# Two fourth sums of a seven-product matrix scheme: from VectorE to accumulating transfers inside SBUF

## The chip, the cores and the metric

The kernel runs on one core of one Trainium2 chip. The core has TensorE (PE, matrix products into PSUM), VectorE (DVE, elementwise work), ScalarE (ACT, activations and copies), GpSimd (POOL, which here issues transfers that add to their target) and SyncE (SP, which issues the other transfers). Transfers from both queues run on the same 16 transfer engines. SBUF is the on-chip memory that all engines work in. The metric is the time on the device in microseconds (us), the median of several executions; lower is better.

## The reference

A two-layer graph attention network over 32 independent graphs of 512 nodes with 512 features, in float32:

```python
h = relu(layernorm(x))
mask = (adj > 0) | eye
# one layer: H heads of F features
xl   = (h @ W).reshape(B, N, H, F)
e    = leaky_relu(asrc[:, :, None] + adst[:, None, :], 0.2)   # asrc, adst: xl against two vectors
attn = softmax(where(mask, e, -1e9), axis=1)
out  = einsum('bsdh,bshf->bdhf', attn, xl) + bias
# layer 1: 4 heads of 256, then elu;  layer 2: 1 head of 512;  result: x + layer 2
```

For every graph that makes four large pieces of matrix work: the first projection (512 x 512 by 512 x 1024), the first gather (four heads, 512 x 512 by 512 x 256), the second projection (512 x 1024 by 1024 x 512) and the second gather (512 x 512 by 512 x 512). The rest is elementwise: the masked softmax, elu, the layer norm and the residual.

## The kernel before, in words

All matrix work is float32, with 128 partitions. Most of it uses a scheme of seven products instead of eight for a product of two 2 x 2 block matrices. Its left factors are a11, a12, a21, a22 and the sums s1 to s4, its right factors b11 to b22 and the sums t1 to t4. The *fourth sums* are s4 = a12 - s2 and t4 = b21 - t2. Product 3 reads s4 and b22, product 4 reads a22 and t4; product 6 reads s2 and t2, product 2 reads a12 and b21.

The pieces that the change touches, by their names in the code:

- `sums` makes s1, s2, the difference for product 7, and s4 of a left factor on DVE. It serves the first projection (`ht`, half the depth), the second projection (`h1`, depth `KH` = 4 blocks, 128 x 1024 elements a sum) and the second gather (the attention weights `p`, 128 x 512 a sum). s4 mostly has no room of its own and is written over s2, which is possible only once both units of product 6 have read s2; the function `last` kept in `left[0]` does that, and `sevens` calls it after the last product 6.
- `sums2` makes t1, t2, the difference for product 7 and t4 of the second gather's right factor, which is the projected features `xl2`. The three sums t1, t2, t4 lie in three buffers of the pool `xs` (four buffers of 128 x 512, which otherwise hold the rows of x that are loaded).
- `sevens` issues the products of one such piece in a given order. An order is a list of pairs (unit, product), a unit being one block of 128 rows: `TWO` for the second projection (four matmuls of 257 columns a product and unit), `NEAR` for the second gather (two matmuls of 256 columns a product and unit). Each matmul stands as two records in the trace.
- `sums_of_weights`, `low_weights`, `low_sums` and `sums1` make such sums for the weights, for a corner of the first projection and for the first gather, on DVE.

For the graph `i` the main loop does, in PE's order: half of the first gather of graph `i+1`, half of the first projection of `i+2`, the other halves, the second gather of `i`, the second projection of `i+1`. The second gather of the last graph is done in the plain way. So there are 32 second projections and 31 second gathers by the scheme.

No engine's order is written by hand but PE's: the functions record jobs (`pe`, `act`, `dve`, `dma`, `accumulate`) with a cost, what they read and what they write. `Program.order` keeps PE's order as recorded, and lays out the jobs of the other engines with a model of the engines and of the two transfer queues, trying ranks until PE's gaps in the model no longer shrink. Then all jobs are issued in that order, each engine working its own in sequence. Each of these helpers issues from one line: L646 is ACT, L649 DVE, L652 a transfer on SP, L657 an accumulating transfer on POOL, L663 PE; so the tile names tell the work apart. Before the change the accumulating transfers serve one purpose: adding the mask (`dm`, bf16 in DRAM) to the attention scores (`p`, f32), two per head. The transposes of the normalized rows (`x<-adj`) are transfers on SP.

The functions that the diff touches, and their callers:

Of the kernel before, what the change touches and what calls it, by code (L numbers as in the profile page):

```python
# [512 lines left out]
def tile_gat(  # L513
# [36 lines left out]
    nc = tc.nc  # L550
# [10 lines left out]
    KH = FT // 2  # L561
# [10 lines left out]
    def slots(name, n, shape, dtype=F32, pool=sbuf):  # L572
        return Slots(name, tiles(name, n, shape, dtype, pool))
# [30 lines left out]
    xs = slots("x", NT, [P, D])  # L604
# [43 lines left out]
    def dve(cost, reads, writes, f, *a, **k):  # L648
        prog.add("DVE", cost, reads, writes, lambda: f(*a, **k))  # L649
# [4 lines left out]
    def accumulate(size, reads, writes, to, at, cost=0.95):  # L654
        prog.add(
            "POOL", cost, reads, writes,
            lambda: nc.gpsimd.dma_start(to, at, accum_op=OP.add), size,  # L657
        )
# [17 lines left out]
    def sums_of_weights(w_sb, keys, cost):  # L676
        b11, b21, b22, t4, t1, t2, t3 = (w_sb[:, i] for i in range(7))
        sub = nc.vector.tensor_sub
        dve(cost, keys(6) + keys(0), keys(4), sub, t1, t3, b11)
        dve(cost, keys(2) + keys(4), keys(5), sub, t2, b22, t1)  # L680
        dve(cost, keys(2) + keys(6), keys(6), sub, t3, b22, t3)
        dve(cost, keys(1) + keys(5), keys(3), sub, t4, b21, t2)

    R01, R_KEYS = w1_sb[:, 1, 0, 1, :], w1_keys(1)

# [420 lines left out]
    M = N // 2  # L1106

    def hs_keys(i, k0, k1):
        return [("hs", i, k) for k in ((0,) if k0 == 0 else ()) + tuple(range(max(k0, KQ), k1))]
# [8 lines left out]
    def sums(blocks, kh, cost, at=0, place=None, keys=None):  # L1118

        a11, a12, a21, a22 = (blocks[r, c] for r, c in ((0, 0), (0, 1), (1, 0), (1, 1)))  # L1120
        if place is None:
            s1, s2 = ((hs[:, i, at : at + kh], hs_keys(i, at, at + kh)) for i in range(2))
            s4 = (hs4, [("hs", 2, 0), ("hs", 2, 1)]) if kh == KQ and at == 0 else s2
        else:
            s1, s2, s4 = (
                (place[:, i].rearrange("p (k m) -> p k m", m=M), keys) for i in range(3)
            )

        def op(f, to, u, v):
            dve(cost, u[1] + v[1], to[1], f, to[0], u[0], v[0])  # L1130

        op(nc.vector.tensor_add, s1, a21, a22)
        op(nc.vector.tensor_sub, a21, a11, a21)
        op(nc.vector.tensor_sub, s2, s1, a11)
        left = {1: a11, 2: a12, 3: s4, 4: a22, 5: s1, 6: s2, 7: a21}

        def last():
            op(nc.vector.tensor_sub, s4, a12, s2)

        if s4 is s2:  # L1140
            left[0] = last
        else:
            last()
        return left
# [25 lines left out]
    def sevens(left, right, rkeys, put, kh, units, width, order, seeds={}):  # L1170


        bank, sixth = {}, len({u for u, _ in order})
        for u, n in order:
            m = units[u][0]
            acc, first = ACC[n], n in (1, 2, 5)
            if first:
                bank[u, acc] = banks.take(width, M if n in seeds else 0)
            bk, bt = bank[u, acc]
            ps = bt[:, :width]  # L1180
            if first and n in seeds:
                first = False
                act(0.29, [seeds[n][1]], [bk], ps, seeds[n][0], AF.Copy)
            a, akeys = left[n]
            pe(
                akeys + rkeys(n), [bk], kh * width / 593,
                [
                    (mm, (ps, a[:, k, m * P : (m + 1) * P], right(n, units[u], k)),
                     dict(start=(first and k == 0), stop=(k == kh - 1), skip_group_check=True))
                    for k in range(kh)  # L1190
                ],
            )
            put(n, units[u], bk, ps)
            if n in (2, 3, 4):
                banks.give(bk)
            sixth -= n == 6
            if n == 6 and not sixth and 0 in left:
                left[0]()
            yield

    TWO = (
        (0, 1), (1, 1), (1, 2), (1, 5), (0, 6), (1, 6), (0, 2), (0, 5), (0, 7), (1, 7), (1, 3), (0, 3),
        (0, 4), (1, 4),
    )
    LAST = (
        (0, 1), (1, 1), (0, 5), (1, 5), (0, 6), (1, 6), (0, 3), (1, 3), (0, 7), (1, 7), (0, 2), (1, 2),
# [171 lines left out]
    def sums1(h, pk, p, apart):  # L1380


        def a_block(i, j):
            return (
                xl[:, 2 * j : 2 * j + 2, h, 2 + i * P : 2 + (i + 1) * P],
                [("xl", 2 * j + k, h, i) for k in range(2)],
            )

        def b_block(r, c):
            return (  # L1390
                p[:, 2 * r : 2 * r + 2, c * M : (c + 1) * M], p_keys(pk, (2 * r, 2 * r + 1), (c,))
            )

        a11, a12, a21, a22 = (a_block(i, j) for i in range(2) for j in range(2))
        b11, b12, b21, b22 = (b_block(r, c) for r in range(2) for c in range(2))
        k = KQ + h % 2
        s1, s2 = (
            (hs[:, i, k, :].rearrange("p (k f) -> p k f", f=P), [("hs", i, k)]) for i in range(2)
        )
        s4 = s2  # L1400
        if apart:
            s4 = (hs4[:, h % 2, :].rearrange("p (k f) -> p k f", f=P), [("hs", 2, h % 2)])
        t1, t2 = (
            (t.rearrange("p (k f) -> p k f", f=M), [q]) for q, t in (ts_.take() for _ in range(2))
        )

        def op(cost, f, to, u, v):
            dve(cost, u[1] + v[1], to[1], f, to[0], u[0], v[0])

        add, sub = nc.vector.tensor_add, nc.vector.tensor_sub  # L1410
        op(0.34, add, s1, a21, a22)
        op(0.59, sub, t1, b12, b11)
        op(0.34, sub, s2, s1, a11)
        op(0.59, sub, t2, b22, t1)
        op(0.34, sub, a21, a11, a21)
        op(0.59, sub, b12, b22, b12)
        if apart:
            op(0.34, sub, s4, a12, s2)
        return (
            {1: a11, 2: a12, 3: s4, 4: a22, 5: s1, 6: s2, 7: a21},  # L1420
            {1: b11, 2: b21, 3: b22, 4: b21, 5: t1, 6: t2, 7: b12},
            lambda: op(0.59, sub, b21, b21, t2),
            (lambda: None) if apart else (lambda: op(0.34, sub, s4, a12, s2)),
        )


# [75 lines left out]
    def x2_key(b, t, c):  # L1502
        return ("x2", b, t, c) if b >= B - LATE else ("xl2", t, c)
# [50 lines left out]
    def sums2(b, soft, place=None, keys=None):  # L1554

        pk, p = soft.p[0]
        blocks = half_blocks(p, KQ, lambda r, c: p_keys(pk, (2 * c, 2 * c + 1), (r,)))
        left = sums(blocks, KQ, 0.59, KQ, place, keys)
        v = x2(b)
        b11, b12, b21, b22 = (  # L1560
            (
                v[:, 2 * r : 2 * r + 2, c * W2H : c * W2H + M],
                [x2_key(b, 2 * r + i, c) for i in range(2)],
            )
            for r in range(2) for c in range(2)
        )
        t1, t2, t4 = (
            (t.rearrange("p (k f) -> p k f", f=M), [k]) for k, t in (xs.take() for _ in range(3))
        )

        def op(to, a, c):
            dve(0.59, a[1] + c[1], to[1], nc.vector.tensor_sub, to[0], a[0], c[0])

        op(t1, b12, b11)
        op(t2, b22, t1)
        op(b12, b22, b12)
        op(t4, b21, t2)
        return left, {1: b11, 2: b21, 3: b22, 4: t4, 5: t1, 6: t2, 7: b12}

    NEAR = tuple((u, n) for n in (1, 5, 6, 2, 7, 3, 4) for u in range(2))  # L1580

    def gather2(b, soft, blocks, order=NEAR):
        left, right = blocks
        xr = XR.pop(b)
        upper = [2, 2]

        def put(n, u, bk, ps):
            r, c = BLOCK[n - 1]
            d = 2 * r + u[0]
            place, xk, xt = xr[d]  # L1590
            to = xt[:, c * M : (c + 1) * M]
            dve(ADD, [bk, xk + (c,)], [xk + (c,)], nc.vector.tensor_tensor, to, ps, to, op=OP.add)

            upper[u[0]] -= n in (2, 3)
            if n == 4 or r == 0 and upper[u[0]] == 0:
                upper[u[0]] = -1
                dma(0.65, [xk, xk + (0,), xk + (1,)], (), out[b, d * P : (d + 1) * P, :], xt)
                place.give(xk)

        yield from sevens(  # L1600
            left, lambda n, u, k: right[n][0][:, k, :], lambda n: right[n][1], put, KQ,
            [(0,), (1,)], M, order,
        )
        ps_.give(soft.p.pop(0)[0])
        for n in (4, 5, 6):
            xs.give(right[n][1][0])

    def gather2_plain(b, soft):
# [93 lines left out]
    for i in range(B - 1):  # L1702
# [17 lines left out]
        if front:  # L1720
# [6 lines left out]
            n = S1[i + 2] = Soft(i + 2, 1, scores_1)  # L1727
# [73 lines left out]
```

## Time and profile before

| What | Value |
|---|---|
| time, median of 3 runs | 2752.51 us (2750.7 to 2756.27) |
| profiled execution, span from first to last instruction | 2756.9 us (the profile gives no other time of that execution) |
| mean granted TensorE clock | 0.999 |
| PE busy | 2732.9 us, 99% |
| DVE busy | 2595.0 us, 94% |
| ACT busy | 2281.9 us, 83% |
| POOL busy | 326.5 us, 12% |
| transfers | 502.10 MB, mean 182 GB/s |

In the rows below, a name such as `hs<-h,hs` is output and inputs by the program's tile names with buffer numbers left out: `hs` holds the sums of left factors, `h` the output of the first layer, `xl` the projected features (of either layer), `x` the pool `xs`, `p` the attention scores, `mm` PSUM, `w_sb` the weights (and, at the end, what is laid over them). A row of groups gives shape, count, busy us and mean ns of one, and after the second bar the idle time of the engine before them. A row of waits gives engine, releaser, us in total, times and the longest.

### The profile page before, as it was taken

The page shows a single profiled execution, that of the slowest core. Times are in us where ns is not written, and L with a number is a line of the kernel's source. Part 1 is how long each engine was busy: PE and PEld are TensorE (multiplying, and loading weights), DVE is VectorE, ACT ScalarE, POOL GpSimd, SP SyncE. Part 2 cuts the span into 40 slices and gives each one's busy share as a digit, 9 for nine tenths or more (in the row PEclk, how much of TensorE's full clock was granted, in tenths as well). Part 3 has the DMA queues.
Part 4 walks back from the last instruction along what each step waited for, and adds up shares of the span by engine and source line. Part 5 has one row for each costly group of instructions (what it writes and reads, how often), then busy time and mean ns, then how long its engine had stood idle before and what let it go on. Part 6 is the DMA issues. An engine that isn't in the chain of part 4 may idle for free.

```text
span 2756.9 us, 41901 instructions
## 1 busy us (share of the span) xinstructions
PE 2732.9 (99%) x12490; PEld 2367.0 (86%) x12490; DVE 2595.0 (94%) x6744; ACT 2281.9 (83%) x4871; POOL 326.5 (12%) x356
## 2 busy tenths in 40 slices
PE   7999999999999999999999999999999999999999
PEld 6688888888888888888888888888888888888887
DVE  8999999999999999999999999999999999999996
ACT  5978898888888888988889887888888898888973
POOL 0111110101111011111011110111111111101110
PEclk9999999999999999999999999999999999999999
DMA  8756866667676677666776666766666766777663
GB/s 225 182 162 181 206 177 173 182 182 194 174 193 176 177 184 206 179 168 183 187 207 173 182 176 183 191 188 182 178 182 180 213 173 172 185 183 199 169 169 108
DMA packets 375863, 502.10 MB, mean 182 GB/s; under 512 B 222804, under 2 KB 227668, under 8 KB 375636
## 3 DMA queue, kind: packets, MB, share of 16 engines
q1 hardware_dynamic: 329844, 332.68, 43.3%
q0 software_dynamic: 45792, 166.74, 24.7%
q8 instruction: 100, 1.64, 0.2%
q14 instruction: 127, 1.04, 0.1%
HBM read 316.41 MB, written 51.31 MB: 133 GB/s over the span
## 4 chain that ended last, share of the span: by engine, by line
PE 97%; DMA 1%; ACT 1%; DVE 0%; SPq 0%; issue 0%; ACTq 0%
PE mm L663 97%; DMA x<-adj 0%; DMA w_sb<-dm 0%; ACT l L646 0%; DMA w_sb<-in_L_gnn_W_dram 0%; DMA as<-das 0%; DMA das<-as 0%; SPq L652 0%; DVE h L649 0%; ACT x L646 0%; DVE hs L649 0%; ACT ht L646 0%; DVE w_sb L649 0%; ACT w_sb L646 0%; DVE xl L649 0%
## 5 line engine op out<-in xcount | busy, mean ns | idle before, releaser
L663 PE MATMUL mm<-w_sb,hs 128*128 128x257 f32 (+2 forms) x3032 | 696.4, 380 | 2.2 <-ACT xl L646 1.6
L663 PEld LDWEIGHTS mm<-w_sb,hs 128*128 128x128 f32 x3032 | 575.3, 190 | 87.7 <-ACT xl L646 2.4
L657 POOL DMA_DIRECT2D p<-dm x314 | 274.3, 878 | 2330.5 <-DVE p L649 1312.6
L646 ACT ACTIVATE l<-l,low 128x512 f32<-128x512 f32 x640 | 458.2, 719 | 23.1 <-DVE low L649 20.6
L663 PE MATMUL mm<-w_sb,h 128*128 128x257 f32 x2056 | 467.9, 379 | 0.0
L663 PE MATMUL mm<-p,xl 128*128 128x256 f32 (+1 forms) x1984 | 466.6, 383 | 0.0
L649 DVE SCALAR_TENSOR_TENSOR p<-rr,z 128x512 f32<-128x512 f32 (+1 forms) x636 | 453.8, 739 | 0.0
L646 ACT ACTIVATE l<-as,z 128x512 f32<-128x512 f32 x640 | 436.7, 714 | 17.4 <-DMA as<-das 16.7
L663 PEld LDWEIGHTS mm<-w_sb,h 128*128 128x128 f32 x2056 | 389.2, 189 | 58.1 <-issue 0.5
L646 ACT ACTIVATE p<-p,z 128x512 f32<-128x512 f32 (+1 forms) x636 | 422.0, 718 | 11.3 <-DVE p L649 8.4
L649 DVE CUSTOM_DVE_ANT_1 l<-l,mt 128x512 f32<-128x512 f32 x640 | 424.8, 681 | 4.4 <-ACT l L646 2.3
L663 PEld LDWEIGHTS mm<-p,xl 128*128 128x128 f32 x1984 | 377.3, 190 | 58.8 <-issue 6.9
L663 PE MATMUL mm<-w_sb,ht 128*128 128x258 f32 x1802 | 419.5, 382 | 2.9 <-ACT ht L646 2.9
L663 PEld LDWEIGHTS mm<-w_sb,ht 128*128 128x128 f32 x1802 | 340.7, 190 | 55.7 <-ACT ht L646 3.3
L646 ACT ACTIVATE h<-mm,b_sb 128x256 f32<-128x256 f32 (+1 forms) x504 | 226.2, 475 | 184.5 <-PE mm L663 183.8
L646 ACT ACTIVATE xl<-mm 128x258 f32<-128x258 f32 (+2 forms) x686 | 258.3, 380 | 84.0 <-PE mm L663 80.6
L649 DVE TENSOR_TENSOR xl<-xl,mm 128x258 f32<-128x258 f32 (+1 forms) x526 | 215.4, 416 | 51.6 <-PE mm L663 47.4
L663 PE MATMUL mm<-t,hs 128*128 128x256 f32 x992 | 226.1, 380 | 0.0
L663 PEld LDWEIGHTS mm<-t,hs 128*128 128x128 f32 x992 | 189.0, 191 | 26.1 <-DVE t L649 0.3
L649 DVE TENSOR_TENSOR t<-mm,t 128x256 f32<-128x256 f32 (+1 forms) x424 | 171.7, 417 | 15.8 <-PE mm L663 13.3
L646 ACT ACTIVATE xr<-h 128x512 f32<-128x512 f32 x256 | 157.6, 624 | 34.5 <-DVE h L649 32.9
L663 PE MATMUL mm<-xl,p 128*128 128x256 f32 (+1 forms) x752 | 179.3, 387 | 0.0
(132 smaller groups left out, 3451.2 us busy)
## 6 DMA issues: line engine op xcount, KB each, us to landing
p<-dm POOLq DMA_DIRECT2D x314, 512.0 KB, 4.9
rr<-drr SPq DMA_DIRECT2D x159, 512.0 KB
x<-in_x_dram SPq DMA_DIRECT2D x129, 256.0 KB
adj<-in_adj_dram SPq DMA_DIRECT2D x128, 256.0 KB
as<-das SPq DMA_DIRECT2D x64, 512.0 KB
t<-in_x_dram SPq DMA_DIRECT2D x124, 256.0 KB
out_dram<-t SPq DMA_DIRECT2D x124, 256.0 KB
dm<-m SPq DMA_DIRECT2D x64, 256.0 KB
```

The source lines that it names most:

```text
L646: prog.add("ACT", cost, reads, writes, lambda: nc.scalar.activation(*a, **k))
L649: prog.add("DVE", cost, reads, writes, lambda: f(*a, **k))
L657: lambda: nc.gpsimd.dma_start(to, at, accum_op=OP.add), size,
L663: f(*a, **k)
```

## The change

s4 of the second projection is no longer subtracted on DVE: with the sign of s2 turned round (s2 = a11 - s1), s4 is a12 + s2, and a transfer issued by POOL adds a12 to s2 in place (128 x 4 x 256 elements, f32, SBUF to SBUF). t4 of the second gather becomes b21 + t2 in the same way (t2 = t1 - b22): a transfer adds t2 to b21 in place (128 x 2 x 256 elements) after the last product 2 has read b21, so t4 needs no buffer of its own, and `xs` gives two buffers instead of three. In `TWO`, products 3 (which read s4) go behind products 4; in `NEAR`, product 2 goes ahead of 5 and 6, so that b21 can be overwritten earlier before product 4, the last. All other sums of the scheme follow the turned sign, with the same number of DVE operations; s4 of the first projection and of the gathers stays on DVE.

```diff
@@ sums_of_weights
-        dve(cost, keys(2) + keys(4), keys(5), sub, t2, b22, t1)
+        dve(cost, keys(2) + keys(4), keys(5), sub, t2, t1, b22)
...
-        dve(cost, keys(1) + keys(5), keys(3), sub, t4, b21, t2)
+        dve(cost, keys(1) + keys(5), keys(3), nc.vector.tensor_add, t4, b21, t2)
@@ sums
-        op(nc.vector.tensor_sub, s2, s1, a11)
+        op(nc.vector.tensor_sub, s2, a11, s1)
         left = {1: a11, 2: a12, 3: s4, 4: a22, 5: s1, 6: s2, 7: a21}
         def last():
-            op(nc.vector.tensor_sub, s4, a12, s2)
+            if kh == KH:
+                accumulate(2.3, a12[1] + s2[1], s2[1], s2[0], a12[0])
+            else:
+                op(nc.vector.tensor_add, s4, a12, s2)
@@ sevens
         bank, sixth = {}, len({u for u, _ in order})
+        second = sixth if len(left[4]) > 2 else 0
...
             if n == 6 and not sixth and 0 in left:
                 left[0]()
+            second -= n == 2
+            if n == 2 and not second and len(left[4]) > 2:
+                left[4][2]()
@@
     TWO = (
-        (0, 1), (1, 1), (1, 2), (1, 5), (0, 6), (1, 6), (0, 2), (0, 5), (0, 7), (1, 7), (1, 3), (0, 3),
-        (0, 4), (1, 4),
+        (0, 1), (1, 1), (1, 2), (1, 5), (0, 6), (1, 6), (0, 2), (0, 5), (0, 7), (1, 7), (0, 4), (1, 4),
+        (1, 3), (0, 3),
     )
@@ sums2
-        t1, t2, t4 = (
-            (t.rearrange("p (k f) -> p k f", f=M), [k]) for k, t in (xs.take() for _ in range(3))
+        t1, t2 = (
+            (t.rearrange("p (k f) -> p k f", f=M), [k]) for k, t in (xs.take() for _ in range(2))
         )
...
         op(t1, b12, b11)
-        op(t2, b22, t1)
+        op(t2, t1, b22)
         op(b12, b22, b12)
-        op(t4, b21, t2)
-        return left, {1: b11, 2: b21, 3: b22, 4: t4, 5: t1, 6: t2, 7: b12}
+        left[4] = (
+            *left[4],
+            lambda: accumulate(1.15, b21[1] + t2[1], b21[1], b21[0], t2[0]),
+        )
+        return left, {1: b11, 2: b21, 3: b22, 4: b21, 5: t1, 6: t2, 7: b12}
-    NEAR = tuple((u, n) for n in (1, 5, 6, 2, 7, 3, 4) for u in range(2))
+    NEAR = tuple((u, n) for n in (1, 2, 5, 6, 7, 3, 4) for u in range(2))
@@ gather2
-        for n in (4, 5, 6):
+        for n in (5, 6):
             xs.give(right[n][1][0])
```

More of the change, by code (lines that the diff above doesn't have):

```diff
@@ L1183, in sevens @@
                 act(0.29, [seeds[n][1]], [bk], ps, seeds[n][0], AF.Copy)
-            a, akeys = left[n]
+            a, akeys = left[n][:2]
             pe(
@@ L1412, in sums1 @@
         op(0.59, sub, t1, b12, b11)
-        op(0.34, sub, s2, s1, a11)
-        op(0.59, sub, t2, b22, t1)
+        op(0.34, sub, s2, a11, s1)
+        op(0.59, sub, t2, t1, b22)
         op(0.34, sub, a21, a11, a21)
@@ L1417, in sums1 @@
         if apart:
-            op(0.34, sub, s4, a12, s2)
+            op(0.34, add, s4, a12, s2)
         return (
@@ L1421, in sums1 @@
             {1: b11, 2: b21, 3: b22, 4: b21, 5: t1, 6: t2, 7: b12},
-            lambda: op(0.59, sub, b21, b21, t2),
-            (lambda: None) if apart else (lambda: op(0.34, sub, s4, a12, s2)),
+            lambda: op(0.59, add, b21, b21, t2),
+            (lambda: None) if apart else (lambda: op(0.34, add, s4, a12, s2)),
         )
```

## The prediction

> **What bounds the kernel now.** I read the page's busy table and the shares of the chain that ended last first, then who TensorE (PE) waited for, then the chain in order of time.
>
> ```profile
> span 2756.9 us, 41901 instructions
> ...
> PE 2732.9 (99%) x12490; PEld 2367.0 (86%) x12490; DVE 2595.0 (94%) x6744; ACT 2281.9 (83%) x4871; POOL 326.5 (12%) x356
> ...
> PE 97%; DMA 1%; ACT 1%; DVE 0%; SPq 0%; issue 0%; ACTq 0%
> ```
>
> ```profile
> PE mm L663 <- ACT x L646: 12.6, 1, 12.6
> PE mm L663 <- ACT ht L646: 2.9, 1, 2.9
> PE mm L663 <- ACT w_sb L646: 1.9, 1, 1.9
> PE mm L663 <- ACT xl L646: 1.6, 1, 1.6
> PE mm L663 <- DVE h L649: 0.6, 1, 0.6
> PE mm L663 <- DVE hs L649: 0.5, 1, 0.5
> ```
>
> ```profile
> 48.92 595.81 PE mm L663 x2674
> 644.73 9.24 DMA x<-adj
> 654.00 1.36 ACT ht L646
> 655.38 0.69 DVE hs L649
> ...
> 662.83 2002.27 PE mm L663 x9232
> 2665.52 7.68 DMA w_sb<-dm
> ```
>
> PE is the bound, almost without a hole. The six rows of its waits are all there are: 20.1 us in 2756.9. The first, 12.6, is the wait for the first inputs, which the change doesn't touch. That leaves 7.5 us: 2.9 at the start (before 48.92), 2.1 (0.5 and 1.6) around 655 to 663, where one transposing transfer needed 9.24 us, and 2.5 near the end. Only 1.1 us of all this was waited for on VectorE (DVE), though DVE is 94% busy: its load is hidden nearly everywhere.
>
> The profiled execution's span is 4.4 us above the median of the runs (2752.51) and 0.6 above the highest of the three (2756.27), so the runs have some of these waits shorter or not at all. If all 7.5 us went, the profiled execution would end at 2749.4, which is 0.1% under the median. This is the ceiling of any gain through less DVE work.
>
> **The change part by part.** *Removed from DVE:* per element of the batch the sum s4 of the second projection, and t4 of the second gather.
>
> ```profile
> L649 DVE TENSOR_TENSOR hs<-h,hs 128x1024 f32<-128x1024 f32 x32 | 39.0, 1218 | 1.3 <-PE mm L663 1.3
> L649 DVE TENSOR_TENSOR x<-xl,x 128x512 f32<-128x512 f32 x60 | 40.9, 682 | 0.0
> L649 DVE TENSOR_TENSOR hs<-p,hs 128x512 f32<-128x512 f32 x29 | 19.7, 678 | 0.0
> ```
>
> The first row is s4: 32 sums, 39.0 us. The second holds t2 and t4 (30 each; the 31st stands under another buffer's name): 31 x 0.682 = 21.1 us. Together 60 us of DVE, 1.9 us per batch element. PE's path gets nothing of it beyond the 1.1 us above. The sign changes (a subtraction turned round, an add for a subtraction) keep shape and count: 0 us.
>
> *Added on POOL:* 32 + 31 = 63 accumulating transfers (POOL goes from 356 instructions to 419). Nothing in this trace adds SBUF to SBUF; the nearest rows are those of the mask sums, p<-dm, which add in the same queue.
>
> ```profile
> L657 POOL DMA_DIRECT2D p<-dm x314: 862/862/1466, 65.3 to 2712.0; - x157
>   ACT p L646: 2.9, 4
> DMA to landing us min/median/max: 4.1/4.9/9.9
> ...
> q1 hardware_dynamic: 329844, 332.68, 43.3%
> q0 software_dynamic: 45792, 166.74, 24.7%
> ```
>
> Queue q0 carried 318 sums (314 and 4 to another buffer). 24.7% of 16 x 2756.9 is 10,895 engine-us: 34.3 each, 2.14 us over 16 engines, in 144 packets of 0.238 us. The fixed part of a sum is then 4.1 - 2.14 = 1.96 us, and traffic stretches the moving part to a median of (4.9 - 1.96) / 2.14 = 1.37 times, at worst 3.7.
>
> s4 writes as many bytes as a mask sum (128 x 1024 f32), t4 half. Lower ends: 2.14 and 1.07 us of moving. Upper ends, if each contiguous piece of 1 KB (512 and 256 of them, and 16 more) takes the 0.238 us of a 4 KB packet: 7.9 and 4.0 us. I take the mask sum scaled by what it takes in: 256 KB of bf16 and 512 of f32 there, 512 and 512 here, so 4/3 x 2.14 = 2.85 us, and 1.43 for t4; same queue, same operation, same bytes written. From issue to arrival: s4 1.96 + 1.37 x 2.85 = 5.9 us, t4 1.96 + 1.37 x 1.43 = 3.9 us.
>
> *Where PE waits for them.* In order of time, one second gather and one second projection on PE:
>
> ```profile
> 1030.33 1.89 PE L663 MATMUL mm<-xl,p 128*128 128x256 f32 x8
> 1032.06 3.61 PE L663 MATMUL mm<-x,hs 128*128 128x256 f32 x16
> ...
> 1040.70 1.89 PE L663 MATMUL mm<-x,p 128*128 128x256 f32 x8
> 1042.42 5.38 PE L663 MATMUL mm<-w_sb,h 128*128 128x257 f32 x24
> 1047.64 5.38 PE L663 MATMUL mm<-w_sb,hs 128*128 128x257 f32 x24
> 1052.86 1.90 PE L663 MATMUL mm<-w_sb,h 128*128 128x257 f32 x8
> ...
> 1059.82 3.64 PE L663 MATMUL mm<-w_sb,hs 128*128 128x257 f32 x16
> 1063.30 3.64 PE L663 MATMUL mm<-w_sb,h 128*128 128x257 f32 x16
> ```
>
> Eight records take 1.73 us (1030.33 to 1032.06), one product of one unit four in the gather (0.865 us), eight in the projection. In the gather t4 may start when the second product 2 has read b21, and the new order 1, 2, 5, 6, 7, 3, 4 leaves 5, 6, 7, 3 for two units, 8 x 0.865 = 6.9 us, until product 4. In the projection s4 may start after the second product 6 (1052.86) and is wanted by product 3, now last (where product 4 began, 1063.30): 10.4 us. A record outlasts the step to the next by 1.89 - 1.73 = 0.16 us; with as much again for the two semaphores 0.3 goes off: 6.6 and 10.1 us. t4 has 2.7 us to spare, s4 4.2. Should the issue grow with the pieces (0.862 to 1.7 and 3.4 us), 0.9 and 2.6 us more still arrive in time. At the worst stretch (3.7) t4 lands at 7.3, 0.7 us late; I grant that to two of the 31: +1.4 us.
>
> *Moved:* products 3 and 4 of the projection change places, product 2 of the gather goes ahead of 5 and 6; PE has the same matmuls: 0 us. Side effects: s2's tile is free 3.5 us later for the sums of the next first gather, whose product 6 comes four products (3.5 us) after the projection; the short DVE sum that writes it fits in (0.68 us for twice its columns, third row above). In the gather the other fourth sum (row hs<-p,hs, 0.68 us) has now 1.73 us between products 6 and 3 instead of 3.45: 0 if at most one short operation stands ahead of it on DVE, a few tenths each if two do. In the built order two residual adds stand ahead, one of which has been released earlier; I take 0. The gather takes one buffer of x fewer, so a load of x can be issued earlier on SP, into t4's stretch: 0 by t4's spare time. Behind t4 and s4 on POOL stand the next mask sums; POOL is 12% busy, and ACT waited only 2.9 us for mask sums in all, so I take 0, the price of lost cover being the second rival.
>
> Sum: 2752.5 + 1.4 = 2753.9, **2754 us**; against the profiled execution's own span 2758, should it keep the wait at 655.
>
> **The rivals.** *1. The SBUF sums go by pieces, not by bytes (slower).* Place: product 4 of each gather, product 3 of each projection. It decides once moving takes over (6.6 - 1.96) / 1.37 = 3.4 us for t4 or 5.9 for s4, 2.4 and 2.1 times what I take. At the upper ends t4 lands at 7.4 (0.8 late), s4 at 12.8 (2.7 late): 31 x 0.8 + 32 x 2.7 = 111 us, 2865; half of it 2809. For it: no such transfer in the trace. Against: q1's packets of mixed, smaller sizes average 0.058 us (43.3% of 44,110 over 329,844), so a packet isn't a fixed price.
>
> *2. A full stretch of the transfer engines gets more (slower).*
>
> ```profile
> core 0: us, PE busy (x) PEld busy (x) DVE busy (x) ACT busy (x) POOL busy (x), PEclk, DMA share, GB/s
> 1033.80:1040.70 6.90, 6.90 (x34) 6.04 (x33) 6.90 (x21) 4.26 (x12) 0.00 (x0) 1.00 0.61 215
> 1052.80:1063.20 10.40, 10.40 (x50) 9.05 (x49) 9.13 (x27) 10.40 (x22) 2.30 (x3) 1.00 1.02 239
> ```
>
> The engines are 61% busy in t4's stretch, but full (1.02) in s4's. There 2.85 us more must push something back: mask sums behind s4 or the transposes that feed the next projection. The latter did stop PE once (9.24 us at 644.73), for 2.1 us. If it happens in 6 of 30 batch elements, 6 x 2.1 = 12.6 us: 2766. It decides from the second on (2753.9 + 4.2). The Trainium skill, "DMA: Bandwidth & Descriptors", section "Queues, rings and completion order", says that an engine takes turns between the queues that have work, packet by packet; by that rule the SP transfers slow down as long as s4 is under way, as this rival has it, and no run here shows the turns. Against it: the instructions were laid out anew with these transfers in.
>
> *3. Less DVE work clears the waits (faster).* At most the 7.5 us: 2745.0 off the median. It needs 5.5 of them to go, and all but 1.1 hang on ACT and transfers.
>
> *4. PE isn't full.* Its weight loads are busy 86%, which leaves 390 us; were waits hidden in it, the 60 us of DVE would come off: 2692. But each run of records above keeps one step, 0.216 us, against a load of 0.19 (2367.0 over 12490), so the 14% is the step's own gap. The Trainium skill, "Trainium Kernel Development and Optimization", section "Performance Expectations", calls matmul busy time a bad metric and weight-load busy a good one; by that rule there is headroom here, and the even step speaks against it.
>
> That the change isn't carried out is excluded: the built program has 63 fewer instructions on DVE and 63 more on POOL.
>
> **How the numbers follow.** No change 0.53 (2754; its own range 2747 to 2758), rival 2 0.26, rival 1 0.14, rival 3 0.05, rival 4 0.02. Within 0.2% means 2747.0 to 2758.0, about what a measurement of this kernel can tell from none. Faster 0.07 (3 and 4), same 0.53, slower 0.40. The range 2747 to 2785 leaves out rivals 3 and 4 (0.07) and most of rival 1 (0.11).
>
> **What would show it.** Right: POOL rows hs<-h x32 and xl<-x x30 with arrivals near 5.9 and 3.9 us; DVE busy near 2535; PE's waits still a handful, under 12 us beside the first; none on POOL's transfers longer than 1 us. Wrong: rows "PE <- DMA hs<-h" or "PE <- DMA xl<-x" by the dozen (rival 1), or PE waits on ACT ht, ACT p or DVE hs in many batch elements behind late x<-adj or p<-dm (rival 2).

## The result, and the profile after

The changed kernel takes 2772.78 us (median of four runs, 2768.97 to 2774.07), the kernel before in the same measurement 2753.47 (2750.70 to 2756.27). The ratio is 1.0066, with a 95% interval of 1.0053 to 1.0078: slower by 0.66% by this ratio, and by 19.3 us between the medians. The forecast value was 2754, with 2747 to 2758 for "no change" and 2747 to 2785 as the range over the rivals: the time lies inside that range and 19 us above the value. The profiled execution of the changed kernel has a span of 2770.6 us, that of before 2756.9. A run's time is 1.8 us longer than its span (2772.42 against 2770.6), so this execution of before was some 5 us longer than the median run, and the two traces show 13.7 us of the 19.3. TensorE's granted clock is 0.999 in both, so the clock doesn't make the difference. Among the runs below, one execution (of the kernel with an eighth of the bytes) took 5660.04 us at a granted clock of 0.908 and is left out of its median.

The page of the changed kernel: span, busy times, the two transfer queues, and the shares of the chain that ended last.

```profile
span 2770.6 us, 41965 instructions
...
PE 2741.3 (99%) x12490; PEld 2362.5 (85%) x12490; DVE 2551.6 (92%) x6681; ACT 2278.4 (82%) x4871; POOL 404.9 (15%) x419
...
q1 hardware_dynamic: 329844, 332.68, 42.6%
q0 software_dynamic: 71120, 191.65, 31.7%
...
PE 89%; ACT 3%; DMA 3%; DVE 3%; issue 1%; SPq 0%; POOL 0%; DVEq 0%; ACTq 0%; POOLq 0%
```

DVE has its 63 instructions fewer, POOL its 63 more, and q0 carries 25,328 packets more (71120 against 45792). PE is still busy 99% of the span, but of the chain it holds 89% where it held 97%. So it is now stopped in many more places, each of them short. Who stopped it, in the view of PE's waits (us in total, times, longest):

```profile
PE mm L663 <- ACT x L646: 11.5, 2, 11.2
PE mm L663 <- ACT xl L646: 3.8, 3, 1.8
PE mm L663 <- DVE xl L649: 3.2, 4, 1.4
PE mm L663 <- DVE w_sb L649: 2.6, 1, 2.6
PE mm L663 <- DVE hs L649: 1.2, 2, 0.8
PE mm L663 <- ACT ht L646: 0.6, 1, 0.6
PE mm L663 <- DVE h L649: 0.6, 1, 0.6
PE mm L663 <- DMA w_sb<-x: 0.4, 1, 0.4
PE mm L663 <- DVE t L649: 0.3, 1, 0.3
PE mm L663 <- ACT p L646: 0.3, 1, 0.3
PE mm L663 <- ACT mm L646: 0.3, 1, 0.3
PE mm L663 <- DVE low L649: 0.2, 1, 0.2
PE mm L663 <- ACT later L646: 0.2, 1, 0.2
```

Thirteen rows with 25.2 us stand where six with 20.1 stood. That is 5.1 us of the 13.7. Another 8.4 is in PE's own busy time (2741.3 against 2732.9) for the same 12,490 matmuls: the ends of matmuls are modelled, and a short stop between two of them is counted as a longer matmul. Together that is 13.5, so the whole difference is PE standing still. The starts of the matmuls say the same: the steps that are over 0.1 us longer than the usual step of their shape add up to 28.1 us more than usual after, 14.0 before. PE hardly waits for the new transfers. The only row of theirs is the 0.4 us for `w_sb<-x`, the sum t4 of the last graph that has one, under its other buffer's name. It waits for ACT and DVE, which are less busy than before, so the next question is what these were late for. The accumulating transfers, in the views of POOL's tiles (instructions with the shortest, median and longest issue in ns; who waited for them; time to landing):

```profile
L657 POOL DMA_DIRECT2D p<-dm x314: 859/859/1803, 63.7 to 2726.2; - x157
...
  ACT p L646: 9.0, 12
...
DMA to landing us min/median/max: 4.1/6.2/13.8
...
L657 POOL DMA_DIRECT2D hs<-h x32: 1299/1313/1347, 117.8 to 2716.4; - x32
...
DMA to landing us min/median/max: 5.8/6.1/11.3
...
L657 POOL DMA_DIRECT2D xl<-x x30: 1205/1205/1223, 186.8 to 2731.7; - x30
...
DMA to landing us min/median/max: 4.1/4.8/6.6
```

s4 (`hs<-h`) lands after a median of 6.1 us, t4 (`xl<-x`) after 4.8. The mask sums, unchanged in number and size, now land at 6.2 instead of 4.9, at worst at 13.8 instead of 9.9, and ACT waits for them 12 times and 9.0 us instead of 4 times and 2.9. Nor are they the only ones to be late. From the chain in order of time (start, length, what), the pieces around which PE's runs break off:

```profile
107.86 13.94 DMA x<-adj
...
895.41 4.75 DMA x<-adj
...
1148.84 5.44 DMA x<-adj
1154.36 2.00 ACT adj L646 x2
...
1156.77 9.00 DMA x<-adj
1165.80 1.36 ACT ht L646
1167.18 0.69 DVE hs L649
...
1178.71 403.28 PE mm L663 x1856
...
1587.54 7.81 DMA as<-das
...
1842.93 7.46 DMA as<-das
...
2659.73 7.94 DMA rr<-drr
```

Before, one transposing transfer of 9.24 us was the only one of its kind in the chain. Now there are four, of 13.94, 9.00, 5.44 and 4.75, and beside them the transfers that bring small vectors back through DRAM (`as<-das`, `rr<-drr`). The chain after has 545 pieces, and PE's longest run without a break is 411 us where it was 2002.

### The profile page after: what moved, and what is told of

It is laid out like the page before. It is cut to its first block, busy times and chain, and to the rows that moved or that the text cites. A ratio compares the mean times of both kernels' runs of the same rounds, so it can differ in the third digit from the quotient of the medians.

```text
span 2770.6 us, 41965 instructions
## 1 busy us (share of the span) xinstructions
PE 2741.3 (99%) x12490; PEld 2362.5 (85%) x12490; DVE 2551.6 (92%) x6681; ACT 2278.4 (82%) x4871; POOL 404.9 (15%) x419
## 3 DMA queue, kind: packets, MB, share of 16 engines
q1 hardware_dynamic: 329844, 332.68, 42.6%
q0 software_dynamic: 71120, 191.65, 31.7%
## 4 chain that ended last, share of the span: by engine, by line
PE 89%; ACT 3%; DMA 3%; DVE 3%; issue 1%; SPq 0%; POOL 0%; DVEq 0%; ACTq 0%; POOLq 0%
PE mm L663 89%; ACT l L646 1%; DMA x<-adj 1%; DVE t L649 1%; DMA as<-das 1%; DVE l L649 0%; ACT adj L646 0%; DMA rr<-drr 0%; ACT p L646 0%; DVE hs L649 0%; DVE p L649 0%; ACT xl L646 0%; ACT x L646 0%; DMA drr<-rr 0%; DVE h L649 0%
## 5 line engine op out<-in xcount | busy, mean ns | idle before, releaser
L657 POOL DMA_DIRECT2D p<-dm x314 | 290.5, 976 | 1709.6 <-DVE p L649 1073.7
L663 PE MATMUL mm<-xl,p 128*128 128x256 f32 (+1 forms) x992 | 238.9, 387 | 1.0 <-DVE t L649 0.3
L663 PEld LDWEIGHTS mm<-xl,p 128*128 128x128 f32 x992 | 184.4, 189 | 41.1 <-DVE t L649 7.0
```

## The experiments

Two theories stood against each other. The first: the transfers cost the time, as they hold up others. The second: all engines' orders are laid out anew whenever a job is added or changed, and the new layout is worse, whatever is in it. The runs first split the two, then vary the size of the transfers in one fixed layout, then ask what it is about the transfers. Differences in us are against the kernel before in the same measurement.

**Both sums given back to DVE, the rest of the change kept.**

```diff
-            if kh == KH:
-                accumulate(2.3, a12[1] + s2[1], s2[1], s2[0], a12[0])
-            else:
-                op(nc.vector.tensor_add, s4, a12, s2)
+            op(nc.vector.tensor_add, s4, a12, s2)
...
-            lambda: accumulate(1.15, b21[1] + t2[1], b21[1], b21[0], t2[0]),
+            lambda: dve(0.59, b21[1] + t2[1], b21[1], nc.vector.tensor_add, b21[0], b21[0], t2[0]),
```

> The changed kernel with both fourth sums given back to DVE: turned signs, moved products, t4 in place and one buffer of x fewer stay, only the 63 transfers go. Theory A (the 63 transfers take 4.1 and 2.0 us of the 16 transfer engines per graph and push the other transfers back): back at the kernel before, 2750 to 2757 us. Theory B (the moved products and tighter places for the DVE sums cost the 19 us): stays at 2765 to 2775. A middle value would split the loss.

2761.15 us, ratio 1.0025 (1.0015 to 1.0035): +6.7, between what the two theories expected. A third of the loss is there without one transfer added, two thirds are not: neither theory does alone. The mask sums of this kernel, with nothing new in their queue, also land later than before (4.9) and hold ACT up more:

```profile
  ACT p L646: 12.7, 9
...
DMA to landing us min/median/max: 4.1/5.6/12.5
```

So later mask sums alone don't tell what costs the time: a layout can have them late by itself.

**One of the two sums as a transfer.** The first kernel has the second hunk of the diff above (t4 back on DVE, s4 a transfer), the second kernel the first hunk.

> The changed kernel with s4 of the second projection by transfer and t4 on DVE. Theory A: the share of the transfer time, 4.1 of 6.1 us per graph, so about 13 of the 19 us: 2766. Theory B: as the kernel with both sums on DVE, whatever that gives.

> The changed kernel with t4 of the second gather by transfer and s4 on DVE. Theory A: 2.0 of 6.1 us per graph, and in a stretch that had room (61% busy): about 6 of the 19 us or less, 2754 to 2760. Theory B: as the kernel with both sums on DVE.

s4 alone as a transfer: 2777.56 us, 1.0079 (1.0066 to 1.0091), +23.2. t4 alone: 2768.33, 1.0050 (1.0038 to 1.0062), +13.9. The first theory had expected 2766 and 2754 to 2760; both came out higher. Each is slower than the kernel with neither. s4 costs more than t4, as its size would have it, but the two excesses over +6.7 (16.5 and 7.2) don't add up to that of both together (12.6). Each of the four kernels has a layout of its own, so a kernel that leaves a sum out can't be read to better than the 6 us or so by which two layouts of the same jobs differ (below).

**The layout of the changed kernel, with smaller transfers.** The jobs and their prices stay, so every engine has the same instructions in the same order; only the bytes of the new transfers shrink: in one kernel to an eighth (of t4 a quarter), called the eighth below, and in another to a half. The rest of each sum is left out.

```diff
-                accumulate(2.3, a12[1] + s2[1], s2[1], s2[0], a12[0])
+                accumulate(2.3, a12[1] + s2[1], s2[1], s2[0][:, 0:1, :M // 2], a12[0][:, 0:1, :M // 2])
...
-            lambda: accumulate(1.15, b21[1] + t2[1], b21[1], b21[0], t2[0]),
+            lambda: accumulate(1.15, b21[1] + t2[1], b21[1], b21[0][:, 0:1, :M // 2], t2[0][:, 0:1, :M // 2]),
```

For the half: `s2[0][:, 0:2], a12[0][:, 0:2]` and `b21[0][:, 0:1], t2[0][:, 0:1]`.

> The changed kernel with each of the 63 transfers moving one piece of 512 bytes per partition instead of its 4 or 2 pieces of 1 KB (an eighth or a quarter of the bytes: this part of the sums is left out). The order of instructions on every engine is that of the changed kernel to the last row. Theory A: most of the 19 us gone, 2750 to 2758, x<-adj and p<-dm landing as before (medians 3.6 and 4.9 us). Theory B or a loss in the new order of instructions: 2768 to 2774.

> The changed kernel, same order of instructions on every engine, each of the 63 transfers moving half of its pieces (half of these sums is left out). With an eighth or a quarter of the bytes the time was 2761.9, with all 2772.8. If the loss follows the time that the transfers take (some 4.1 and 2.0 us of moving at full size), half of them gives 2765 to 2769. If it came from a few transfers that pass a limit, 2761 to 2764 or still 2771 and up.

An eighth: 2760.90 us (median of the other seven runs), 1.0029 (1.0018 to 1.0040), +6.5; with the first theory alone 2750 to 2758 was expected, with the second 2768 to 2774. A half: 2763.93, 1.0035 (1.0021 to 1.0049), +8.9, at the border of the two cases that were expected (2761 to 2764, 2765 to 2769). Whole: +19.3. The intervals of the whole and of the half lie apart. So in one and the same order of instructions 12.8 us by the medians, 10.2 by the ratios, come with the size of the transfers; what is left at an eighth is about the same as in the kernel without transfers. By the medians most of the cost comes with the second half. But the half's interval reaches up to +13.5, and a cost in proportion to the bytes would give about +11.6 there, so that isn't excluded. With an eighth the tiles of POOL show:

```profile
L657 POOL DMA_DIRECT2D p<-dm x314: 862/862/1214, 61.9 to 2714.3; - x157
...
  ACT p L646: 3.9, 3
...
DMA to landing us min/median/max: 4.1/5.5/10.3
...
L657 POOL DMA_DIRECT2D hs<-h x32: 864/912/1446, 112.9 to 2700.5; - x32
...
DMA to landing us min/median/max: 2.4/4.4/10.2
```

The mask sums land at 5.5, between before (4.9) and the whole change (6.2), and ACT's waits for them are 3.9 us, near those of before.

As the order is the same, the traces of the eighth and of the whole can be compared matmul by matmul. From the first matmul to the last the whole falls 13.3 us behind. 1.9 of this comes before the first new transfer is issued, and so isn't its doing but scatter between executions. 2.7 comes near 122 us, 1.0 near 900, 3.1 near 1170, 1.7 near 1855 and 2.2 near 2660 (times of the whole); all the rest makes 0.7. So the size costs time at a few places, and in most graphs nothing. Where the whole stops at the first four, the eighth runs through:

```profile
48.84 117.57 PE mm L663 x478
...
864.16 248.26 PE mm L663 x1142
...
1118.78 454.04 PE mm L663 x2090
...
1597.12 530.95 PE mm L663 x2446
```

The transfers compare one by one as well, from issue to landing. Of those in the chain after, all of SP's queue, the transpose at 107.86 took 13.94 us where the same one took 10.65 in the eighth, that at 1156.77 9.00 against 4.51, `as<-das` at 1842.93 7.46 against 5.67, `rr<-drr` at 2659.73 7.94 against 6.18; the transpose at 895.41 was hardly longer (4.75 against 4.67). The median of all 120 transposes is 3.5 us with an eighth, 3.8 with a half and 4.4 with the whole, against 3.6 before. So larger transfers in POOL's queue make transfers of the other queue longer: not only what stands behind them on POOL is late.

**Other seeds of the layout.** The search that lays the jobs out draws random numbers. Another seed gives the same work in another order, in the kernel before and in the changed one:

```diff
-        chance = Random(1)
+        chance = Random(2)
```

> The kernel before with the random numbers of its layout search started from 2 instead of 1: the same work, another order of instructions on the engines beside PE. With both sums back on DVE 7 us of the loss stayed; theory B1 (any new layout costs some us against the one that the kernel before has) expects 2757 to 2765 here; theory B2 (the moved products cost the 7 us) expects 2752 to 2757.

> The changed kernel with the search started from 2. Theory A (transfer time) with B1: as far above the kernel before as the changed kernel, give or take the scatter of layouts, 2766 to 2780; if it came at or below 2760, the loss would be mainly the layout that was drawn.

Before with the other seed: 2760.37 us, 1.0024 (1.0014 to 1.0034), +6.6 with nothing else changed. The changed kernel with the other seed: 2773.27, 1.0068 (1.0056 to 1.0081), +19.5. So the order that the kernel before happens to have is worth 6.6 us more than another draw for the same jobs, and both draws of the changed kernel lie some 13 us above that other draw. The waits of PE in the reseeded kernel before:

```profile
PE mm L663 <- ACT x L646: 12.7, 1, 12.7
PE mm L663 <- DVE hs L649: 4.1, 1, 4.1
PE mm L663 <- ACT ht L646: 3.1, 2, 2.7
...
```

One wait of 4.1 us for a sum of the left factors is the new row in it; before, that sum cost 0.5.

**The old orders of products, with both sums on DVE.** On top of the first experiment, `TWO` and `NEAR` as before. What remains of the change is the turned signs, t4 in place and the buffer of x saved.

```diff
-        (0, 1), (1, 1), (1, 2), (1, 5), (0, 6), (1, 6), (0, 2), (0, 5), (0, 7), (1, 7), (0, 4), (1, 4),
-        (1, 3), (0, 3),
+        (0, 1), (1, 1), (1, 2), (1, 5), (0, 6), (1, 6), (0, 2), (0, 5), (0, 7), (1, 7), (1, 3), (0, 3),
+        (0, 4), (1, 4),
...
-    NEAR = tuple((u, n) for n in (1, 2, 5, 6, 7, 3, 4) for u in range(2))
+    NEAR = tuple((u, n) for n in (1, 5, 6, 2, 7, 3, 4) for u in range(2))
```

> Both sums on DVE as in the first experiment, and also the old orders of products in the second projection and the second gather: of the change only the turned signs, t4 in place and one buffer of x fewer are left. Theory B2: 2752 to 2757. Theory B1: 2757 to 2765, as with the new orders.

2758.08 us, 1.0016 (1.0007 to 1.0025), +4.3. Even this, with every product and sum where it was, is slower than before, by about what a draw of the layout costs. Against the first experiment (+6.7) the moved products may account for 2.4 us, but the intervals overlap, and two draws differ by more.

**s4 in long pieces.** What is it about the size? The transfer of s4 consists of 512 pieces of 1 KB. Here it is 128 pieces of 4 KB with the same bytes, in the same layout.

```diff
-                accumulate(2.3, a12[1] + s2[1], s2[1], s2[0], a12[0])
+                accumulate(
+                    2.3, a12[1] + s2[1], s2[1], s2[0].rearrange("p k m -> p (k m)"),
+                    h1[:, KH : KH + 2, :].rearrange("p k n -> p (k n)"),
+                )
```

> The changed kernel, same order of instructions, the s4 transfer moving as many bytes but in 128 pieces of 4 KB instead of 512 of 1 KB (it reads a contiguous part of h1, not a12, so the sum is another one). Packets of 4 KB took 0.264 us in the mask sums, those of 1 KB 0.127: s4 would take 2.1 instead of 4.1 us of moving and its issue 0.86 instead of 1.31. If time on the engines is what costs, about a third of the 11 us that hang on the bytes goes: 2766 to 2770. If bytes alone count, 2771 to 2775.

```profile
q0 software_dynamic: 58832, 191.65, 30.8%
...
L657 POOL DMA_DIRECT2D hs<-h x32: 861/867/930, 116.3 to 2715.1; - x32
...
DMA to landing us min/median/max: 4.7/5.0/11.2
```

2773.38 us, 1.0067 (1.0053 to 1.0081), +18.4. The issue is shorter by a third (0.87 against 1.31 us) and s4 lands 1.1 us earlier, and no time comes back (18.4 against 19.3, with intervals that cover each other). It lies in the 2771 to 2775 that were expected if the bytes alone count. So neither the longer issue of s4 nor a microsecond of s4's own length is what costs.

**Room on the common engines.** If the sum of all transfer time is too much for the 16 engines, then taking time off another queue must help. For the rows whose place is `ts_`, only 64 of 512 columns of the residual are loaded and of the result stored, on SP, in the same layout.

```diff
-            dma(0.8, [x2_key(b, 0, 0)], halves, xr, x[b, d * P : (d + 1) * P, :])
+            n = 64 if places[d] is ts_ else N
+            dma(0.8, [x2_key(b, 0, 0)], halves, xr[:, :n], x[b, d * P : (d + 1) * P, :n])
...
-                dma(0.65, [xk, xk + (0,), xk + (1,)], (), out[b, d * P : (d + 1) * P, :], xt)
+                n = 64 if place is ts_ else N
+                dma(0.65, [xk, xk + (0,), xk + (1,)], (), out[b, d * P : (d + 1) * P, :n], xt[:, :n])
```

> The changed kernel, same order of instructions, all 63 transfers whole, but the loads of the residual rows and the stores of the result on SP move 64 of 512 columns for 31 of the 32 graphs (the rest of the output is left out). That takes some 4.5 us per graph off the 16 engines (8 transfers of 128 packets of 2 KB at 0.097 us, against 256 B at 0.027), against 6.1 us that the new transfers put on. Theory A1 (what costs is the time of the common engines, whichever queue has it): 2760 to 2767. Theory A2 (what costs is POOL's queue alone: the mask sums behind s4 and the longer issues): 2770 to 2775.

2776.86 us, 1.0084 (1.0071 to 1.0097), +23.2, above both ranges that were expected (2760 to 2767, 2770 to 2775). The queues of this kernel, and one row of the view by windows, for the changed kernel first and then for this one (us, busy time of PE, PE's loads, DVE, ACT, POOL, then clock, share of the transfer engines, GB/s):

```profile
q1 hardware_dynamic: 329844, 276.71, 36.9%
q0 software_dynamic: 71120, 191.65, 31.8%
```

```profile
100.00:2600.00 2500.00, 2490.66 (x11436) 2162.01 (x11435) 2326.45 (x6008) 2107.12 (x4502) 373.29 (x382) 1.00 0.76 192
```

```profile
100.00:2600.00 2500.00, 2491.05 (x11431) 2162.53 (x11430) 2327.05 (x6009) 2106.44 (x4501) 373.32 (x383) 1.00 0.70 170
```

The engines' share falls from 0.76 to 0.70, and PE gets through no more matmuls in the same 2500 us (11,431 records against 11,436). The total time of the engines over the whole run is therefore not what is short. But most of the room came where no s4 is under way: over the 32 stretches from the second product 6 to the place of product 3 in the new order, the engines' share is 0.94 on average in the changed kernel and 0.90 in this one, against 0.83 with an eighth and 0.90 before. So the run doesn't settle whether full engines in those stretches cost the time. In its trace the two transposes of 13.94 and 9.00 us are down to 9.93 and 5.85, and ACT's waits for mask sums to 5.1 us; other stops stand in their place, the longest, 4.0 us, behind a transpose of 10.41 us issued at 1584.48. The Trainium skill, "DMA: Bandwidth & Descriptors", section "Queues, rings and completion order", has an engine take turns between queues with work, which the second rival drew on; no run here shows the turns, and this one shows that fewer bytes in the other queue, taken off where these were, bring no time back.

**The search told the longer times.** In the program's model s4 counts 2.3 us of moving and t4 1.15, the price of a mask sum and half of it; on the chip they take about 4.2 and 2.1 (below). One kernel gives the model the longer times and issues, with 20 tries of the search in place of 100; its control is the changed kernel with 20 tries.

```diff
-    MARK, SIGHT, TRIES, BACK = 20, 80, 100, 5.0
+    MARK, SIGHT, TRIES, BACK = 20, 80, 20, 5.0
...
-                accumulate(2.3, a12[1] + s2[1], s2[1], s2[0], a12[0])
+                accumulate(4.3, a12[1] + s2[1], s2[1], s2[0], a12[0], 1.4)
...
-            lambda: accumulate(1.15, b21[1] + t2[1], b21[1], b21[0], t2[0]),
+            lambda: accumulate(2.15, b21[1] + t2[1], b21[1], b21[0], t2[0], 1.3),
```

> The changed kernel with the layout search told what the transfers really take (s4 4.3 and t4 2.15 in place of 2.3 and 1.15, issues 1.4 and 1.3 in place of 0.95), with 20 tries per gap instead of 100. If the loss came from the layout not knowing the length of the new transfers, the loss against the next kernel of this call is 4 us smaller or more; if the added time itself costs, it is the same within 3.

> The changed kernel with 20 tries per gap instead of 100 and nothing else, to compare the one before with: 2768 to 2780, as the changed kernel with the scatter of layouts.

The control: 2769.65 us, 1.0058 (1.0044 to 1.0072), +15.9. Told: 2803.19, 1.0175 (1.0158 to 1.0193), +49.5. The row that changed most in PE's waits, in the control and in the kernel that was told:

```profile
PE mm L663 <- DVE hs L649: 7.8, 3, 4.3
```

```profile
PE mm L663 <- DVE hs L649: 14.8, 11, 3.4
```

Telling the search more truly made the kernel 33.5 us slower, which neither theory expected. That the loss comes from a layout made for transfers of half their real length is tempting, since transfers of half the bytes, about as long as the model believes, cost little by the medians (+8.9 against +6.5); but this run doesn't bear it out. It doesn't exclude it either, as the search may simply have ended in a worse place. ACT waits only 2.3 us for mask sums in the slowest kernel of all, and 12.7 in the one with both sums on DVE: across the kernels, the time doesn't follow these waits. No version tried beats the kernel before.

## Why the forecast value missed and the range held, step by step

- *The base, 2752.5.* This step failed first, and no term of the sum stood for it: the time of before was carried over although all engines' orders were drawn anew. The rival about full engines was even discounted because "the instructions were laid out anew with these transfers in". Four kernels without new transfers, or with an eighth of them, stand at +4.3, +6.5, +6.6 and +6.7; one of them is the kernel before with another seed. So some 6 of the 19.3 us are the price of leaving an order that happened to be good. That rests on two draws for the kernel before and two for the changed one; how wide such draws scatter was not measured.
- *"Behind t4 and s4 on POOL stand the next mask sums ... I take 0".* This term failed too, and it is the larger one. In the fixed layout the size of the transfers is worth 19.3 - 6.5 = 12.8 us, 10.2 by the ratios. That is near the 12.6 that the second rival put on it, and so is the form: five places with 1.0 to 3.1 us each instead of six with 2.1, three of them with a transpose in the chain, the others with a transfer through DRAM. The agreement is partly luck: "6 of 30" was a guess, its 2.1 us were read from one place, and nothing in the prediction says which graphs would stop.
- *The mechanism of that rival*, full transfer engines while s4 is under way, is not settled. The stretch it was read from (1.02) is not the usual one: of the 32 before, five are at 1 or above and the mean is 0.90. 156 us of the engines' time given back (42.6% of 2770.6 less 36.9% of 2774.8) regained nothing, but came mostly at other times. What is shown is that transfers on SP grow with the bytes on POOL's queue, so waiting in line on POOL isn't the whole cause. Which neighbours s4 and t4 meet, and whether it is the engines that they share, stays open; the run with long pieces says that a microsecond less of s4 isn't enough.
- *The range, 2747 to 2785.* It held because it was kept wide for rivals 1 and 2. No rival had the drawn order in it; the rival's 2766 and those 6 us happen to add up to the time measured.
- *Moving time, 2.85 and 1.43 us.* Too small. q0 took 31.7% of 2770.6 us after and 24.7% of 2756.9 before: 197 us more for 32 s4 and 31 t4 of half the size, so 4.2 and 2.1 us. This lies between what was taken and the upper ends (7.9 and 4.0). The issue of 0.862 us was 1.31 and 1.21, within the bounds named. The arrivals, forecast at 5.9 and 3.9, were 6.1 and 4.8: less stretch than assumed made up for the size of s4.
- *"The SBUF sums go by pieces" (first rival).* By the place it named, refuted: PE waits for neither product 3 nor product 4, and 4.2 us stays under the 5.9 from which it would decide. The spare times worked out from PE's records held. The 1.4 us for two late t4 came to 0.4.
- *DVE's 60 us at nothing, and the ceiling.* Right in that PE got nothing of it. DVE is busy 43.4 us less, not 60 (31.0 with s4 alone taken off, 14.2 with t4 alone). The 60 added up the lengths of records, and records of operations in sequence overlap: before, all their lengths come to 3091.5 us against 2595.0 busy. PE got nothing of the 43.4, so that less DVE work clears waits, and that PE has hidden room, are both out.
- *Moved products at 0.* Not contradicted: the run with the old orders is 2.4 us below that with the new ones, less than two draws of the layout differ.

What the prediction named as showing it wrong, waits on ACT and DVE behind late `x<-adj`, is in the trace, but at a few places and not in many batch elements. PE's waits beside the first came to 14.0 us in 19 stops, where it had put under 12 in a handful as a sign of being right.

## What to carry to other kernels

Where one engine is busy 99% of the time, taking work off another buys at most the few waits on it, while each added transfer can make something else late. If a search lays the kernel out, build the unchanged kernel once more with another seed before reading a difference: here that alone was worth 6.6 us, about a third of the result. And to see what transfers cost, shrink them in the same order of instructions rather than taking them out.

## What the runs showed of the hardware that was not expected

- An accumulating transfer from SBUF to SBUF in pieces of 1 KB took 0.125 us a packet (3,158 us of the engines' time over the 25,328 added packets, from the shares above), about half of the 0.238 of a mask sum's packet: the price goes neither by the piece nor by the byte. In the long form of s4 the same reckoning, with t4 at 2.1 us, leaves 3.4 us a sum, 0.37 us a packet of mostly 4 KB.
- The issue on POOL grows with the pieces: 0.87 us for 128, 1.21 for 256, 1.31 for 512.
- In one order of instructions, larger transfers in POOL's queue made the transposes in SP's queue longer: a median of 3.5, 3.8 and 4.4 us to landing with an eighth, a half and the whole.
- Taking records of 60 us off DVE lowered its busy time by 43.4 us. Overlap of the records is a part of it; whether it is all was not tried. With both sums back on DVE its busy time is 2595.0, as before.
